# A two-layer MetaFormer on one core: the second layer's order taken from a table of 59 operations by one rule, instead of a repeated period of 34 steps

## The chip, the cores and the metric

The kernel runs on one core of a Trainium2 chip. The time is that of the device for one execution, in microseconds; the number compared is the median of several runs. The engines named below are PE (matrix multiply), DVE (vector), ACT (activations), POOL (GpSimd), and SP, which only issues transfers. Each engine works through its own list of instructions in the order in which the program emitted them, and an instruction whose operands aren't ready stops everything behind it on that engine.

## What is computed

The input is 16 samples of 128 channels by 32 x 32 positions. Cut to what matters:

```python
# layer 0
x = x + linear_attention(ln_c(x))            # GroupNorm, q/k softmax, 4 heads
t = t + stu(ln_t(t))                          # spectral filters over the 1024 tokens: FFT convolutions + 3 taps
# layer 1
h = ln_c(x)                                   # normalize over channels, per position
x = x + relu(bn(conv3x3(relu(bn(conv3x3(h, w1))), w2)) + h)
n = ln_t(tokens(x))                           # normalize over channels, per token
p = softmax(n @ gate_w.T, over tokens)        # 64 experts choose
vals, idx = top_k(p, 8)                       # 8 tokens per expert
pooled = sum over k of vals * n[idx]
out = gelu([pooled, 1] @ weight1) , then @ weight2   # per expert
x = x + scatter_add(out * vals at idx)        # back to the chosen tokens
```

## The kernel before

Layer 0 has two stages (attention and the forward transform for all samples; then the products with the spectral filters, in 16 chunks of 8 frequencies each). Each chunk leaves results in DRAM (`yd`, L839). Layer 1 runs per sample b and is what the change touches. A sample goes through these steps, each a handful of instructions:

- **Inverse transform.** The sample's `y` is loaded from `yd` and its `x` from `xd` (`load`, L960 to L963). POOL forms the even classes (L976, L977), DVE the odd sums, turns and classes (L983 to L1003), PE multiplies by the inverse table `wi` (L1045), and DVE adds the result to x (L1053).
- **First norm.** PE transposes x into PSUM (L149), ACT copies the tile to `tok` (L1059), DVE takes the moments with four bn_stats (L132) from the same PSUM tile, ACT takes logarithm and exponential for the inverse root (L118, L119), POOL refines it and forms the shift (L1020 to L1027), ACT normalizes eight blocks (L141), PE transposes back (L159), and ACT copies the image into a padded tile `pads` (L1070).
- **Two 3 x 3 convolutions**, in a form that computes two output columns from four products. DVE forms four terms (L920). For each half of the rows, PE computes a "middle" pair of products and an "outer" pair (12 matmuls each, L926) into one of three PSUM tiles; ACT shifts (L936), DVE forms sums (L938, L939) and rows (L946, L947). After the first convolution ACT applies the relu into `pads` (L1080); after the second DVE adds the residual and x (L1091, L1093).
- **Second norm and routing.** Tokens again (L1103 for the copy), moments, root, scales, norm, a transpose to channels (L159, L1116). Then once per pair of samples: logits (L1125, L1130), the eight largest (L1135, L1137), marks (L1139), exponential (L1142), gates (L1146), a transpose of the gates (L1156) and the pooling (L1162 to L1171).

The transposes, the inverse transform, the logits and the turned gates share a PSUM tile `big` with two buffers; the products share `pcv` with three. `y` has two buffers, `z`, `zt`, `tok` and the logits tile one, the term tile `v` two, the image two, the relu's image one.

A sample is a Python generator, `convolve_and_route(b)`, that yields at 34 named points. The order is a list `period` of (name, offset): in period p the step `name` of sample p + offset is emitted, so that a period of the steady state holds steps of seven different samples. Its first six entries and the loop:

```python
period = (
    ("first0", 0), ("pooled", -4), ("scales2", -2), ("largest", -3), ("first0o", 0),
    ("norm2", -2), ...
)
for p in range(-2, B + 4):
    for name, d in early if p < 0 else period:
        b = p + d
```

The instructions of these engines keep the order in which they are emitted. In a step, everything stays together: "tokens" is transposes, then ACT's copy, then the moments; "first0" is the middle products, the shift and the sums. After the last sample's pooling the experts' stage begins (L1226 on), whose weights `we` are loaded into buffers that layer 1 gives up (`load_half`).

Of the kernel before, what the change touches and what calls it, by code (L numbers as in the profile page):

```python
# [66 lines left out]
def metaformer_kernel(ctx: ExitStack, tc: tile.TileContext, io: dict, out: bass.AP):  # L67
# [60 lines left out]
    def moments(work, src):  # L128

        bst = work.tile([P, NT, 3], F32, name="bst", tag="bst", bufs=4)  # L130
        for j in range(0, NT, 2):
            nc.vector.bn_stats(  # L132
                bst[:, j : j + 2, :].rearrange("p j s -> p (j s)"),
                src[:, j : j + 2, :].rearrange("p j c -> p c j"),
            )
        return bst[:, :, 1], bst[:, :, 2]
# [27 lines left out]
    with ExitStack() as l0:  # L164
# [6 lines left out]
              for i, n in enumerate((P - JL, JL))]  # L171
# [574 lines left out]
        with ExitStack() as g0:  # L746
# [61 lines left out]
            for c in range(NCH):  # L808
# [27 lines left out]
                for kl in range(JL // RG):  # L836
                    last = c + 1 == NCH
                    j0 = kl * RG + (0 if last else c * JL)
                    nc.sync.dma_start(  # L839
                        yd[last][j0 : j0 + RG].rearrange("g r b x e -> (g r b) (x e)"),  # L840
                        ys[:, kl].rearrange("p x m e -> p (x m e)"),
                    )
# [12 lines left out]
    with ExitStack() as c1:  # L855
# [76 lines left out]
        def conv_middle(v, wt, hf, bias):  # L932

            pc = products(v, wt, hf, (1, 2))
            t = work.tile([P, HR, WT], F32, name="ct", tag="ct")
            nc.scalar.activation(t, pc[:, 0], AF.Identity, bias=bias)  # L936
            sd = work.tile([P, 2, HR, WT], F32, name="cs", tag="cs")
            nc.vector.tensor_tensor(sd[:, 0], pc[:, 1], t, ALU.add)  # L938
            nc.vector.scalar_tensor_tensor(sd[:, 1], pc[:, 1], -1.0, t, ALU.mult, ALU.add)  # L939
            return sd  # L940

        def conv_outer(v, wt, hf, sd):

            pc = products(v, wt, hf, (0, 3))
            r = work.tile([P, 2, HR, WT], F32, name="r", tag="r")
            nc.vector.tensor_tensor(r[:, 0], pc[:, 0], sd[:, 0], ALU.add)  # L946
            nc.vector.scalar_tensor_tensor(r[:, 1], pc[:, 1], -1.0, sd[:, 1], ALU.mult, ALU.add)  # L947
            return r

# [8 lines left out]
        def load(b):  # L958
# [3 lines left out]
            for i, js in enumerate((slice(P - JL), slice(P - JL, P))):  # L962
                (nc.gpsimd if b + i == 0 else nc.sync).dma_start(  # L963
                    yts[b][js].rearrange("p r x e -> p r (x e)"),
                    yd[i][:, :, b].rearrange("j r x e -> j r (x e)"),
                )
# [43 lines left out]
        def convolve_and_route(b):  # L1010

            pr, j = divmod(b, 2)
            p1, p2 = pads[:, b % 2], pads[:, 2]
            g = nc.gpsimd

            def scales(q, e):

                sts = work.tile([P, 5, NT], F32, name="sts", tag="sts")
                r, a, t, mm, nm = (sts[:, i, :] for i in range(5))
                g.tensor_scalar(a, q, 1.0 / C, e, ALU.mult, ALU.add)  # L1020
                log_exp(r, q, 1.0 / C, e)
                g.tensor_tensor(t, r, r, ALU.mult)
                g.tensor_tensor(t, t, a, ALU.mult)
                g.tensor_scalar(t, t, -0.5, 1.5, ALU.mult, ALU.add)
                g.tensor_tensor(r, r, t, ALU.mult)
                g.tensor_scalar(mm, r, -1.0, None, ALU.mult)
                g.tensor_tensor(nm, m, mm, ALU.mult)  # L1027
                return r, nm


            xb = xt[b]
            y = yts.pop(b).rearrange("p r x e -> p (r x) e")
            z = work.tile([P, 12, C], F32, name="z", tag="z", bufs=1)
            even_classes(z, y)
            zt = odd_sums(y)
            yield "classes"
            odd_turns(*zt[1:])
            yield "classes2"
            odd_classes(z, zt[0], zt[2])
            yield "classes3"  # L1040
            px = big()
            for q in range(NQ):
                for r in range(2):
                    zq = y[:, q // 4 + 2 * NM * r, :] if q % 4 == 0 else z[:, 2 * ZQ[q] + r, :]
                    nc.tensor.matmul(  # L1045
                        px[:, q * P : (q + 1) * P], zq, wi[:, q, r, :],
                        start=(r == 0), stop=(r == 1),
                    )
            del y
            if b + 1 < B:  # L1050
                load(b + 1)
            xv = xb.rearrange("p (s q) -> p s q", q=NQ)
            nc.vector.tensor_tensor(xv, px.rearrange("p (q s) -> p s q", q=NQ), xv, ALU.add)  # L1053
            yield "inverse"

            pt = tokens(big())
            transpose_in(pt, xb)
            tok = work.tile([P, NT, C], F32, name="tok", tag="tok", bufs=1)
            nc.scalar.copy(tok, pt)  # L1059
            m, q = moments(work, pt)  # L1060
            yield "tokens"
            r, nm = scales(q, 1e-6)
            yield "scales"
            normalize(tok, tok, r, nm, 0, 2)
            yield "norm0"
            normalize(tok, tok, r, nm, 2, NT)
            yield "norm1"
            px = big()
            transpose_out(px, tok)
            nc.scalar.copy(inner(p1), px.rearrange("p (h w o) -> p o h w", w=WT, o=2))  # L1070
            yield "image"
            v = first.tile([P, 4, HP, WT], F32, name="v", tag="v", bufs=2)
            terms(v, p1, (1, 2, 0, 3))
            yield "terms"
            for hf in range(2):
                sd = conv_middle(v, cw[0], hf, bn[:, 0, 1:2])
                yield f"first{hf}"
                r = conv_outer(v, cw[0], hf, sd)
                yield f"first{hf}o"
                nc.scalar.activation(inner(p2, hf), r, AF.Relu)  # L1080
                yield f"first{hf}r"
            v = first.tile([P, 4, HP, WT], F32, name="v", tag="v", bufs=2)
            terms(v, p2, (1, 2))
            yield "terms2"
            terms(v, p2, (0, 3))
            yield "terms3"
            for hf in range(2):
                sd = conv_middle(v, cw[1], hf, bn[:, 1, 1:2])
                yield f"second{hf}"
                r = conv_outer(v, cw[1], hf, sd)  # L1090
                nc.vector.tensor_tensor(r, r, inner(p1, hf), ALU.add)  # L1091
                xh = xb[:, hf * HALF : (hf + 1) * HALF].rearrange("p (n o) -> p o n", o=2)
# [3 lines left out]
                yield f"second{hf}o"  # L1096


            pt = tokens(big())
            transpose_in(pt, xb)  # L1100
            tt = work.tile([P, NT, C], F32, name="tt", tag="tt", bufs=4)
            toks[b] = tt
            nc.scalar.copy(tt, pt)  # L1103
            m, q = moments(work, pt)
            yield "tokens2"
            r, nm = scales(q, 1e-5)
            yield "scales2"
            normalize(tt, tt, r, nm, 0, 3)
            yield "norm2"
            normalize(tt, tt, r, nm, 3, NT)  # L1110
            yield "norm3"
            pu = big()
            transpose_out(pu, tt)
            tk = work.tile([P, N], F32, name="tk", tag="tk")
            tks[b] = tk
            nc.scalar.copy(tk, pu)  # L1116
            yield "channels"
            if j == 0:
                return

            pl = big()
            for hf in range(2):
                cs = slice(hf * HALF, (hf + 1) * HALF)
                for jj in range(2):
                    nc.tensor.matmul(  # L1125
                        pl[jj * E : (jj + 1) * E, cs], gw, tks[b - 1 + jj][:, cs],
                        start=True, stop=True, skip_group_check=True,
                    )
            lg = work.tile([P, N], F32, name="lg", tag="lg", bufs=1)
            nc.scalar.activation(lg, pl, AF.Identity, bias=gb)  # L1130
            yield "logits"


            top = work.tile([P, TOPK], F32, name="top", tag="top")
            nc.vector.max(top, lg)  # L1135
            lr = work.tile([P, N], F32, name="lr", tag="lr", bufs=1)
            nc.vector.match_replace(lr, top, lg, -3.0e38)  # L1137
            yield "largest"
            nc.vector.tensor_tensor(lr, lg, lr, ALU.not_equal)  # L1139
            ss = work.tile([P, 3], F32, name="ss", tag="ss")  # L1140
            nc.vector.tensor_scalar(ss[:, 0:1], top[:, 0:1], -1.0, None, ALU.mult)
# [251 lines left out]
```

## Time and profile before

| | |
|---|---|
| Time, median of 3 runs | 1379.61 us (1378.31 to 1382.88) |
| PE busy over the span | 1242.8 us, 90% |
| DVE, ACT, POOL busy | 920.6 (67%), 700.1 (51%), 486.7 us (35%) |
| PE's last product of layer 0 / first of layer 1 | ends 679.3 / starts 693.5 us |
| Experts' first matmul | 1270.4 us |
| DMA | 162.98 MB, mean 118 GB/s |

The page is that of one profiled execution; times within it are microseconds from its start. Busy time of an engine is the sum over its instructions, and "idle before" is the time for which an engine stood still ahead of an instruction, with the event that ended it. A share over the whole span mixes the three stages, so stretches of the trace are looked at by themselves.

### The profile page before, as it was taken

The page shows a single profiled execution, that of the slowest core. Times are in us where ns is not written, and L with a number is a line of the kernel's source. Part 1 is how long each engine was busy: PE and PEld are TensorE (multiplying, and loading weights), DVE is VectorE, ACT ScalarE, POOL GpSimd, SP SyncE. Part 2 cuts the span into 40 slices and gives each one's busy share as a digit, 9 for nine tenths or more (in the row PEclk, how much of TensorE's full clock was granted, in tenths as well). Part 3 has the DMA queues.
Part 4 walks back from the last instruction along what each step waited for, and adds up shares of the span by engine and source line. Part 5 has one row for each costly group of instructions (what it writes and reads, how often), then busy time and mean ns, then how long its engine had stood idle before and what let it go on. Part 6 is the DMA issues. An engine that isn't in the chain of part 4 may idle for free.

```text
span 1379.3 us, 33751 instructions
## 1 busy us (share of the span) xinstructions
PE 1242.8 (90%) x14116; PEld 1000.6 (73%) x14116; DVE 920.6 (67%) x1982; ACT 700.1 (51%) x1424; POOL 486.7 (35%) x816
## 2 busy tenths in 40 slices
PE   4889999999989999999659998989998999976885
PEld 4767777777768888888557987878787888852343
DVE  4788878787756766667446877777777767652224
ACT  4777767776556666666213444444454444433111
POOL 2233544546576777777411111111111111100002
PEclk7899999999999999999979999999999999986898
DMA  6015333342443333333662214040404033015895
GB/s 257 16 34 164 110 131 122 123 149 92 154 161 103 126 127 129 129 126 118 215 160 46 47 31 104 5 107 1 107 1 107 1 92 122 16 65 200 314 368 244
DMA packets 87274, 162.98 MB, mean 118 GB/s; under 512 B 5457, under 2 KB 40657, under 8 KB 86737
## 3 DMA queue, kind: packets, MB, share of 16 engines
q1 hardware_dynamic: 86449, 158.27, 34.9%
q0 software_dynamic: 672, 2.56, 0.6%
q8 instruction: 111, 1.82, 0.5%
q14 instruction: 42, 0.34, 0.1%
HBM read 104.18 MB, written 56.62 MB: 117 GB/s over the span
## 4 chain that ended last, share of the span: by engine, by line
PE 34%; DVE 8%; ACT 4%; DMA 2%; issue 1%; POOL 1%; POOLq 0%; SPq 0%; ACTq 0%; DVEq 0%
PE pcv L926 19%; PE big L1045 4%; PE big L149 2%; PE big L159 2%; PE big L1125 1%; PE ph L1233 1%; PE pp L1162 1%; PE peo L1257 1%; PE ph L1226 1%; DMA we<-in_weight 1%; DVE bst L132 1%; ACT tt L141 1%; DVE v L920 1%; DVE lr L1137 1%; ACT lg L1142 1%
## 5 line engine op out<-in xcount | busy, mean ns | idle before, releaser
L926 PE MATMUL pcv<-v,cw 128*128 128x256 f32 x1536 | 347.5, 385 | 1.9 <-DVE v L920 1.9
L926 PEld LDWEIGHTS pcv<-v,cw 128*128 128x128 f32 x1536 | 293.3, 194 | 42.6 <-DVE v L920 2.1
L785 ACT COPY g<-pg 128x512 f32<-128x512 f32 x288 | 153.1, 591 | 101.7 <-PE pg L776 101.7
L783 DVE COPY g<-pg 128x512 f32<-128x512 f32 x224 | 145.9, 687 | 87.4 <-PE pg L776 87.4
L776 PE MATMUL pg<-ph,mst 32*128 32x128 f32 x4096 | 154.2, 286 | 4.5 <-ACT g L785 3.1
L776 PEld LDWEIGHTS pg<-ph,mst 32*128 32x128 f32 x4096 | 129.7, 189 | 30.7 <-issue 25.6
L1020 POOL TENSOR_SCALAR sts<-bst 128x8 f32<-128x8 f32 x32 | 11.9, 371 | 394.5 <-DVE bst L132 394.5
L796 PE MATMUL py<-g,v 128*32 128x128 f32 x4096 | 139.0, 276 | 4.3 <-issue 1.4
L132 DVE BATCH_NORM_STATS2 bst<-big 128x6 f32<-128x256 f32 x256 | 91.4, 419 | 55.7 <-ACT tok L1059 29.3
L796 PEld LDWEIGHTS py<-g,v 128*32 128x32 f32 x4096 | 104.8, 109 | 20.8 <-issue 2.7
L767 POOL TENSOR_TENSOR v<-xc 128x256 f32<-128x256 f32 x128 | 92.0, 746 | 69.0 <-PE py L796 60.0
L141 ACT ACTIVATE tok<-tok,sts 128x128 f32<-128x128 f32 x256 | 103.1, 481 | 5.8 <-DVE sts L375 3.3
L920 DVE TENSOR_TENSOR v<-pads 128x544 f32<-128x544 f32 x128 | 86.2, 725 | 7.9 <-ACT pads L1070 6.4
L618 PE MATMUL big<-u,mu 128*128 128x128 f32 (+4 forms) x384 | 86.0, 380 | 0.0
L936 ACT ACTIVATE ct<-pcv,bn 128x256 f32<-128x256 f32 x64 | 30.0, 469 | 91.7 <-PE pcv L926 91.7
L274 POOL TENSOR_TENSOR xf<-ab 128x256 f32<-128x256 f32 x34 | 24.8, 729 | 132.2 <-DVE ab L241 132.1
L938 DVE TENSOR_TENSOR cs<-pcv,ct 128x256 f32<-128x256 f32 x64 | 27.0, 421 | 65.4 <-ACT ct L936 65.3
L618 PEld LDWEIGHTS big<-u,mu 128*128 128x128 f32 x384 | 56.7, 191 | 18.0 <-issue 15.4
L141 ACT ACTIVATE tt<-tt,sts 128x128 f32<-128x128 f32 x128 | 52.5, 482 | 28.3 <-POOL sts L1027 28.3
L1045 PE MATMUL big<-wi,z 128*128 128x128 f32 x384 | 54.2, 294 | 10.0 <-DVE z L1003 7.1
L551 PE MATMUL big<-wf,ub 128*128 128x256 f32 x256 | 62.0, 385 | 0.2
L149 PEld LDWEIGHTS big<-ident,x 128*128 128x128 f32 x384 | 46.9, 148 | 20.9 <-issue 8.1
(230 smaller groups left out, 2284.4 us busy)
## 6 DMA issues: line engine op xcount, KB each, us to landing
we<-in_weight SPq DMA_DIRECT2D x32, 1024.0 KB
vd<-xf SPq DMA_DIRECT2D x16, 1024.0 KB
xc<-vd SPq DMA_DIRECT2D x64, 256.0 KB
yd<-ys SPq DMA_DIRECT2D x32, 512.0 KB
y<-yd SPq DMA_DIRECT2D x15, 960.0 KB
x<-in_x SPq DMA_DIRECT2D x16, 512.0 KB
mi<-in_M_phi SPq DMA_DIRECT2D x16, 512.0 KB
xd<-x SPq DMA_DIRECT2D x16, 512.0 KB
```

Source lines behind the costliest of these rows:

```text
L132: nc.vector.bn_stats(bst[:, j : j + 2, :].rearrange("p j s -> p (j s)"), src[:, j : j + 2, :].rearrange("p j c -> p c j"),)
L141: nc.scalar.activation(dst[:, j, :], src[:, j, :], AF.Identity, bias=nm[:, j : j + 1], scale=r[:, j : j + 1],)
L149: nc.tensor.transpose(pt[:, j, :], src[:, j * P : (j + 1) * P], ident)
L618: nc.tensor.matmul(self.pa[:, a:hi], mu[:, NF - 1 - si, tap, :], self.u[:, a - tap : hi - tap], start=(tap == 0), stop=(tap == KU - 1),)
L767: nc.gpsimd.tensor_tensor(vv[:, x, 1:, bs], e, o, op)
L776: nc.tensor.matmul(pg[r][:, i], mst[rs, 4 * q + i, :], ph[rs, c, :], start=True, stop=True,)
L783: nc.vector.tensor_copy(dst, src)
L785: nc.scalar.copy(dst, src)
L796: nc.tensor.matmul(py[rows, x, kl, :], v[:, (x * NM + m) * JL + jl, 1 - ri : 3 - ri, :] .rearrange("p k b -> p (k b)"), g[:, ((x * 2 + ri) ...
L920: nc.vector.tensor_tensor(v[:, k], d[i], d[j], op)
L926: nc.tensor.matmul(pc[:, i], wt[:, dy, k, :], v[:, k, hf * HR + dy : hf * HR + dy + HR], start=(dy == 0), stop=(dy == 2),)
L1045: nc.tensor.matmul(px[:, q * P : (q + 1) * P], zq, wi[:, q, r, :], start=(r == 0), stop=(r == 1),)
```

## The change

The generator becomes a class `Routed` with one method for each operation of one engine. What was a step with work on three engines is now taken apart: copies, moments, variance, root, products, shifts, sums and relus are operations of their own. A table gives each operation its engine, a duration in us, a due time, the operations it depends on, and the buffers it opens and closes. Before the program is emitted, `planned` goes through all operations of all 16 samples once: of those whose inputs are done (0.15 us later when they come from another engine) and whose buffers are free, it finds the earliest that can start, and among all that can start within 0.25 us of that one it takes the one with the earliest due time (due + 54.66 per sample). The list, sorted by planned start and then by name, is the order of emission. It is thus no longer periodic: the first and the last samples have an order of their own. The samples' inputs are taken to be there at 0, 4 and 8 us for the first three, and always for the others.

Beside it: `load` of two samples is issued at the beginning and that of sample b + 2 with the inverse of b (before: one, and b + 1); the last write group of `yd` holds two chunks (16 rows) instead of one, so that the load of the first 112 rows doesn't depend on chunk 14; the buffers of the moments' tile go from 4 to 5, of the scales' tile from 2 to 4. The aim is to keep PE supplied, in the middle and at both ends, and to take the moments, which the norm waits for, ahead of the copies. The computation is the same. The core of the diff:

```diff
-        bst = work.tile([P, NT, 3], F32, name="bst", tag="bst", bufs=4)
+        bst = work.tile([P, NT, 3], F32, name="bst", tag="bst", bufs=5)
...
-              for i, n in enumerate((P - JL, JL))]
+              for i, n in enumerate((P - 2 * JL, 2 * JL))]
...
-                    last = c + 1 == NCH
-                    j0 = kl * RG + (0 if last else c * JL)
+                    last = c + 2 >= NCH
+                    j0 = kl * RG + (c - NCH + 2 if last else c) * JL
...
-            pt = tokens(big())
-            transpose_in(pt, xb)
-            tok = work.tile([P, NT, C], F32, name="tok", tag="tok", bufs=1)
-            nc.scalar.copy(tok, pt)
-            m, q = moments(work, pt)
-            yield "tokens"
...
+            def tokens(self):
+                self.pt = tokens(big())
+                transpose_in(self.pt, self.x)
+
+            def stats(self):
+                self.m, self.q = moments(work, self.pt)
+                self.sts = small([P, 5, NT], "sts")
+
+            def copy(self):
+                self.tok = work.tile([P, NT, C], F32, name="tok", tag="tok", bufs=1)
+                nc.scalar.copy(self.tok, self.pt)
...
+        table = (
+            ("even", "POOL", 1.85, -409.2, "", "z", ""),
+            ("odd", "DVE", 1.4, 60, "", "zt", ""),
+            ("odd_turn", "DVE", 0.75, -162.8, "odd", "", ""),
+            ("odd_out", "DVE", 1.4, 308, "odd_turn even", "", "zt"),
+            ("inverse", "PE", 3.5, -181.4, "even odd_out", "big:0", "z"),
+            ("add", "DVE", 1.25, 32, "inverse", "", "big:0"),
+            ("tokens", "PE", 0.88, -255.4, "add", "big:1", ""),
+            ("stats", "DVE", 1.4, 65, "tokens", "", "big:1"),
+            ("copy", "ACT", 1.02, -202.6, "tokens", "tok", "big:1"),
...
+            ("terms", "DVE", 2.6, -242.7, "image_copy", "v:0", ""),
+            ("middle 0", "PE", 2.6, -433, "terms", "cv:0m", "v:0"),
+            ("shift 0", "ACT", 0.48, -171, "middle0", "", ""),
+            ("sums 0", "DVE", 0.74, -165.9, "shift0", "cs:0", "cv:0m"),
+            ("outer 0", "PE", 2.6, -360.9, "terms", "cv:0o", "v:0"),
+            ("rows 0", "DVE", 0.74, -387.6, "outer0 sums0", "r:0", "cv:0o cs:0"),
+            ("relu 0", "ACT", 0.64, -76.6, "rows0", "p2", "r:0"),
...
+            ("terms_middle", "DVE", 1.36, -205.6, "relu0 relu1", "v:1", ""),
+            ("terms_outer", "DVE", 1.36, -37.3, "terms_middle", "", "p2"),
...
+            ("logits", "PE", 1.75, -188.7, "channels_copy -channels_copy", "big:5", "tk -tk"),
...
+            ("pooled_copy", "DVE", 0.3, 242, "pooled", "", "s"),
         )
...
+        buffers = dict(z=1, zt=1, big=2, tok=1, p1=2, v=2, cv=3, cs=2, r=2, p2=1, tt=4, tk=2, lg=1, lr=1, gt=1, s=1)
...
+        order = planned(
+            table, buffers, B, 54.66, lambda b, name: b % 2 == 0 and name in pairs,
+            lambda b: 4.0 * b if b < 3 else 0.0,
+        )
...
+            for b in range(2):
+                load(b)
...
+                if b == B - 1 and name == "inverse":
                     for h in range(5):
                         load_half(h)
-                elif p == B:
+                elif b == B - 1 and name == "rows21":
                     for h in range(5, len(RING)):
                         load_half(h)
+                elif b == B - 1 and name == "logits":
...
+    hop, window, never = 0.15, 0.25, 1e18
...
+        soon = min(starts.values()) + window
+        k = min((k for k, t in starts.items() if t <= soon), key=lambda k: (ops[k][2], starts[k]))
...
+    return [k for _, k in sorted(order)]
```

## The prediction

> **What bounds the kernel now.** I first read the stages: busy time of each engine in stretches of the second layer (the two convolutions and the routing, 692 to about 1270 us). The columns are the stretch, its length, busy time of PE, weight loads, DVE, ACT and POOL with instruction counts, granted clock, DMA share, GB/s.
>
> ```profile
> 671.00:692.00 21.00, 5.62 (x166) 4.47 (x160) 4.77 (x12) 1.12 (x3) 4.74 (x6) 0.81 0.90 298
> 692.00:752.00 60.00, 44.84 (x224) 39.03 (x225) 32.90 (x70) 15.97 (x33) 8.80 (x21) 0.81 0.48 111
> 752.00:820.70 68.70, 68.70 (x387) 61.76 (x385) 56.14 (x123) 32.60 (x73) 12.54 (x41) 1.00 0.17 39
> ...
> 886.70:952.70 66.00, 62.53 (x372) 53.72 (x371) 49.50 (x104) 31.02 (x64) 11.19 (x32) 1.00 0.23 57
> ...
> 1151.70:1200.00 48.30, 45.83 (x262) 38.71 (x262) 29.99 (x60) 24.01 (x49) 6.14 (x21) 0.96 0.27 99
> 1200.00:1268.00 68.00, 47.68 (x231) 34.56 (x231) 29.47 (x56) 22.90 (x40) 2.86 (x14) 0.80 0.30 108
> ```
>
> PE bounds the stage: nothing is free from 752 to 820.7, where no routing runs yet. From 820.7 on a pair of samples takes 66.1 us (the logits matmuls start at 820.73 and, four pairs later, at 1085.21), with DVE busy 49.5 us and ACT 31.0 us. The ends are looser than the middle.
>
> Busy PE is not PE at its peak, so I count what a pair must stream, with the back-to-back spacing in the chain that ended last: 192 convolution matmuls at 0.216 us (24 in 5.18) are 41.4; 64 of the inverse transform at 0.112 (32 in 3.57) are 7.1; 72 transposes at 0.109 are 7.8; logits 1.9, pooling 1.9, pooled 0.1. Sum 60.2 us, **5.9 us less than the period**. Where they go, in the order of time on PE (start, length, and in brackets the idle time before it and its releaser):
>
> ```profile
> 904.32 0.49 PE L159 MATMUL big<-ident,tt 128*128 128x128 f32 x3
> 906.24 1.87 PE L159 MATMUL big<-ident,tt 128*128 128x128 f32 x5 [1.43 <-ACT tt L141]
> ...
> 919.18 0.61 PE L1045 MATMUL big<-wi,y 128*128 128x128 f32 x4
> 920.39 1.60 PE L1045 MATMUL big<-wi,z 128*128 128x128 f32 x12 [0.60 <-DVE z L1003]
> ...
> 923.89 1.09 PE L149 MATMUL big<-ident,gt 128*128 128x128 f32 x8
> 926.09 1.09 PE L149 MATMUL big<-ident,x 128*128 128x128 f32 x8 [1.10 <-ACT gtt L1156]
> ```
>
> PE stands ahead of work that isn't ready while other products could run: 3.1 us of plain gaps, and five transposes that take 1.87 us because each waits for its normalized tile. That is a matter of order, which is what is changed. Last, who waits on the engines beside PE in that pair (waiter, releaser, us, times, longest):
>
> ```profile
> ACT ct L936 <- PE pcv L926: 8.1, 4, 3.7
> DVE cs L938 <- ACT ct L936: 7.7, 4, 3.6
> ...
> DVE bst L132 <- ACT tok L1059: 3.6, 2, 2.0
> ```
>
> DVE's moments wait for ACT's copy of the same PSUM tile; over the layer this line stands at 29.3 us, 16 times.
>
> [...] (all 16 moments of the first norm start after the copy's end, 0.03 us later, at 706.10 for the first). [...] after PE's 14.1 us of idleness before 693.5 the granted clock is 0.50 and inverse matmuls take 0.552 instead of 0.275 us. It makes gaps of several us at both ends dearer than they look.
>
> **The change, part by part.** No matmul, vector or ACT instruction is added or removed; one 8-element POOL operation per norm becomes an operation of its own.
>
> *Order in the middle.* The rule starts, on every engine, what is ready first and breaks near ties (0.25 us) by due time. Its table agrees with the trace: 27.8 us of PE per sample and 4.5 per pair make 60.1 (60.2 measured); a product 2.6 (2.59), terms 2.6 (2.63), moments 1.4 (1.43). PE is the fullest queue, and the table's engines are DVE 49 and ACT 31 per pair, so PE rarely lacks something ready: between a sample's two convolutions lies rows, relu and two terms, 0.74 + 0.64 + 1.36 and hops, some 3.2 us, against 7 us of other PE work per sample. Bounds on the saving are 0 and 5.9 us per pair. I take 3.7, to 62.4 a pair: the waits of the fence above less some new ones. Five pairs (820.7 to 1151.7): **18 us**.
>
> *The end.* From 1151.7 to the experts' first matmul at 1270.4 are 118.7 us. Still to stream: 240 convolution matmuls (51.8), 32 inverse (3.6), 105 transposes (11.4), logits and pooling of three pairs (5.6 + 5.7): 78.4 with the rest. From the last convolution's end (1238.1) to 1270.4 runs one chain, tokens, moments, norm, logits, largest eight, gates, pooling; the order can't shorten it, and I leave it at 32 us, of which 9 stream. Before 1238.1 then, 86.4 us hold 69 of work: 17 lost, since the old period thins out as samples run out. With the last samples interleaved freely I keep 6 of them: **11 us**.
>
> *The start.* The last write group now holds two chunks, 16 rows. Before, GpSimd's bulk load of the first sample waited 8.3 us for chunk 14's store, was issued at 683.4, landed at 692.7; the small load followed chunk 15's store (686.5) and PE began at 693.5. Chunk 13's store was issued at 658.0, so the bulk load can now go out near 672 and land beside the weights (4 MB at the 382 GB/s of 671 to 681, over by about 685). The small load doubles to 128 KB but finds less ahead of it: bounds 0 and 5 us, I take **3.5**. From the first convolution (718.9) to 752 the old order holds 25.2 us of streaming in 33.1; I take **4** of the 8.
>
> *Moments ahead of copies.* At equal planned starts the sort falls to the names, and "copy" comes before "stats"; moments go first only where ACT is busy longer than DVE. The plan lets both overlap, the chip does not: whichever is second is late by 1.0 or 1.4 us against the plan, twice per sample. If DVE is second, its queue (sums and rows of the products, which free the three product banks) stands 1 us; PE has up to two products of 2.6 us queued in free banks meanwhile. Bounds 0 and 2 us per sample.
>
> *Loads the plan doesn't know.* After sample 2 the table thinks every sample's input is there at once. But y has two buffers: sample b+2's load is issued when inverse b has read y, and lands about 8 us later (issued 714.9, DMA full until 723). The rule can put DVE's odd sums of b+2 as early as inverse b's end + 0.15 + 1.85 (even) + 0.15 + 1.4 (odd out), 3.6 us after it and 5 us after the issue. So DVE can stand up to 3 us per sample with sums and rows queued behind it; where DVE is backlogged it costs nothing. Bounds 0 and 3 us per sample. For both leaks together I charge 0.5 us per sample, **8 us**: DVE has 12 us of room in 62, and product banks absorb most of it.
>
> *Five moment buffers, split POOL operation, prefetch of two samples:* nothing. Moments wait on copies, not buffers; POOL is busy 11 of 66 us; y loads were issued at the same event before, SP running ahead to the buffer's release.
>
> Sum: 18 + 11 + 3.5 + 4 - 8 = 28.5, less one for a slow-clock stretch: about 27.5 us off 1379.6, **1352 us**. The experts' stage follows rigidly: four of its first nine weight loads are tied to the last sample's rows, 30 us ahead of pooled in both kernels.
>
> **Rivals.** (1) *DVE becomes the bound.* 49.5 busy, plus 4 of copies and up to 6 of loads per pair is 59.5 of 62. Then the middle keeps its 66 us, and only the ends gain, some 11 us: **1369**. For it: the two leaks above; against: a late DVE no longer waits for loads. (2) *Slower.* A fixed order for all samples, worked out with durations, has no slack written into it; if each sample's stall repeats on PE the pair becomes 68 us, 5 x 2 = 10 lost, and the ends give nothing: **1390**. For it: PE had no gap at all from 752 to 820.7, which the new order can only keep or spoil, and inverse transforms run early take PE from products; against: measured products are no longer than the table's, so PE as the bound queue gives the others slack. (3) *Near the floor:* 61 us a pair (26), 14 at the end, 8 at the start, leaks of 4: 44 off, **1336**.
>
> **Chances.** Forecast 0.58, DVE-bound 0.20, slower 0.14, near the floor 0.08. Range 1334 to 1384, which takes in the first rival and the floor, and cuts through the slower case. Faster by over 0.3% (under 1375.5) is the forecast, the floor and nearly all of the first rival less some scatter: 0.81; same 0.05; slower 0.14.
>
> **What would show it.** Right: logits matmuls some 62.4 us apart per pair; waits of PE on ACT tt L141 and gtt copies gone from the middle; first inverse matmul near 690; less than 10 us of idle PE between 752 and the last convolution; the last convolution's end to the experts' first matmul still near 32 us. The leaks show as DVE's zt operations waiting for the y load and as moments still behind copies (or copies behind moments). Wrong: pairs still 66 apart with DVE over 85% busy or waiting (rival 1), or pairs above 66 with PE idle on DVE's terms or rows (rival 2). A moved start of the experts' stage without a moved end would mean that weight loads bound it, which I take not to be so.

## The result, and the profile after

1323.88 us (median of 4 runs, 1323.63 to 1324.34) against 1379.85 before: a ratio of 0.9592, 95% interval 0.9576 to 0.9609. The kernel is 56 us faster, twice what was forecast and 10 us under the low end of the range. One execution among all those reported below, in the kernel with its end filled, took 1599.0 us at a granted clock of 0.74; it counts as slow and is left out.

The stages of the changed kernel, with the columns of the first view of before (stretch, length, busy time of PE, weight loads, DVE, ACT and POOL, granted clock of PE as a share of full speed, DMA share, GB/s):

```profile
694.00:752.00 58.00, 47.51 (x283) 43.14 (x284) 44.99 (x102) 20.22 (x43) 15.03 (x31) 0.88 0.55 144
752.00:813.80 61.80, 60.04 (x337) 53.27 (x335) 43.93 (x97) 28.07 (x60) 13.20 (x32) 1.00 0.20 52
...
874.50:935.20 60.70, 60.70 (x371) 53.39 (x373) 47.47 (x103) 31.86 (x64) 12.89 (x32) 1.00 0.22 62
...
1117.20:1185.00 67.80, 67.80 (x367) 57.40 (x367) 50.53 (x105) 32.18 (x60) 8.31 (x21) 1.00 0.02 9
1185.00:1217.50 32.50, 19.97 (x126) 13.73 (x124) 12.08 (x24) 16.06 (x30) 3.17 (x14) 0.79 0.62 227
1217.50:1322.00 104.50, 79.91 (x920) 38.63 (x920) 34.08 (x62) 13.61 (x20) 9.42 (x4) 0.94 0.84 322
```

A pair takes 60.7 us, half a microsecond more than the 60.2 counted as PE's streaming work; PE has no gap from 799 to the end of the last product (1187.6). The same place in a pair as was shown of before, in the order of time on PE, carries no bracket any more:

```profile
899.86 1.04 PE L159 MATMUL big<-ident,tt 128*128 128x128 f32 x8
900.73 1.04 PE L149 MATMUL big<-ident,gt 128*128 128x128 f32 x8
901.60 2.76 PE L926 MATMUL pcv<-v,cw 128*128 128x256 f32 x12
904.29 1.97 PE L1242 MATMUL pp<-tt,gtt 128*64 128x128 f32 x32
906.19 1.09 PE L159 MATMUL big<-ident,tok 128*128 128x128 f32 x8
```

The eight channel transposes stream in 1.04 us, since they start when all eight blocks are normalized, and a product of 2.6 us stands between the gates' transposes and the pooling, where before PE waited 1.1 us for ACT's copy.

Where the 57.1 us between the two profiled executions (1379.3 and 1322.2) lie, by the starts of matmuls:

| Stretch | before | after | gain |
|---|---|---|---|
| to the end of layer 0 | 679.3 | 681.3 | -2.0 |
| end of layer 0 to first inverse matmul | 14.1 | 13.5 | 0.7 |
| to the first logits | 127.2 | 119.0 | 8.2 |
| five pairs, first to sixth logits | 331.0 | 303.4 | 27.6 |
| sixth logits to the experts' first matmul | 118.7 | 100.4 | 18.3 |
| experts and output | 109.0 | 104.7 | 4.3 |

Layer 0's end lies between 677.4 and 681.6 in the twelve profiles without added matmuls at that place, whose code there differs at most in loads and stores; so I take its 2 us for scatter.

### The profile page after: what moved, and what is told of

Read it like the earlier page. It is cut to its first block, busy times and chain, and to the rows that moved or that the text cites. A ratio compares the mean times of both kernels' runs of the same rounds, so it can differ in the third digit from the quotient of the medians.

```text
span 1322.2 us, 33734 instructions
## 1 busy us (share of the span) xinstructions
PE 1216.7 (92%) x14116; PEld 990.8 (75%) x14116; DVE 907.2 (69%) x1982; ACT 705.2 (53%) x1424; POOL 503.3 (38%) x816
## 5 line engine op out<-in xcount | busy, mean ns | idle before, releaser
L926 PE MATMUL pcv<-v,cw 128*128 128x256 f32 x1536 | 342.9, 380 | 0.0
L926 PEld LDWEIGHTS pcv<-v,cw 128*128 128x128 f32 x1536 | 286.8, 190 | 42.2 <-issue 5.7
L141 ACT ACTIVATE tok<-tok,sts 128x128 f32<-128x128 f32 x256 | 101.8, 481 | 23.8 <-POOL sts L1001 20.4
L1066 POOL TENSOR_SCALAR sts<-bst 128x8 f32<-128x8 f32 x16 | 6.5, 406 | 235.7 <-DVE bst L132 235.7
L149 PE MATMUL big<-ident,x 128*128 128x128 f32 x384 | 53.6, 286 | 8.5 <-DVE x L1048 3.4
L1115 DVE TENSOR_TENSOR r<-pcv,cs 128x256 f32<-128x256 f32 x64 | 26.9, 420 | 49.0 <-PE pcv L926 48.2
L141 ACT ACTIVATE tt<-tt,sts 128x128 f32<-128x128 f32 x128 | 51.1, 480 | 9.2 <-POOL sts L1001 8.9
```

The costliest lines, as they stand in the source:

```text
L141: nc.scalar.activation(dst[:, j, :], src[:, j, :], AF.Identity, bias=nm[:, j : j + 1], scale=r[:, j : j + 1],)
L149: nc.tensor.transpose(pt[:, j, :], src[:, j * P : (j + 1) * P], ident)
L926: nc.tensor.matmul(pc[:, i], wt[:, dy, k, :], v[:, k, hf * HR + dy : hf * HR + dy + HR], start=(dy == 0), stop=(dy == 2),)
```

## The experiments

Theory A: PE's own order, with DVE's and ACT's operations placed so that its operands are there, makes the gain. Rivals: B, DVE's waits on copies had held PE back; C, the loads at the start; D, a plan passes every delay on to PE. A later question was what in the plan does it: the rule, the lengths or the due times.

The kernel before, measured anew beside the experiments, took 1382.9, 1383.9 and 1383.7 us, 3 to 4 us more than beside the change. So a time below is to be compared with the changed kernel's by the two ratios, or by lengths of stretches inside the traces; a difference of a few us between two times says nothing.

**Moments ahead of copies, alone, in the kernel before.**

```diff
-            nc.scalar.copy(tok, pt)
             m, q = moments(work, pt)
+            nc.scalar.copy(tok, pt)
```
(and the same for `tt`)

> The kernel before with one edit: in both norms the moments are emitted ahead of ACT's copy of the same tile. If the whole gain came from the order of PE's work (theory A), the 41 us of DVE waits on copies go, copies wait for moments instead, and the time stays within 6 us of 1380. If DVE's waits on copies were what held PE back (theory B, a rival), most of the 5.9 us per pair goes and the time falls by 20 us or more, to 1360 or less.

Measured 1373.2, ratio 0.9937 (0.9914 to 0.9961): 9 us off, 64.5 us per pair in four of its five pairs. Between the two expectations. Waits in one pair of it (waiter, releaser, us, times, longest):

```profile
ACT tt L1104 <- DVE bst L132: 8.5, 2, 5.5
...
ACT tok L1060 <- DVE bst L132: 1.3, 2, 0.8
```

The copies now wait for moments, for longer than the moments had waited for them (3.6 and 1.3 us in that pair of before), and still PE gains 1.6 us per pair. Its waits for the second norm (ACT tt L141, 7.1 us over five pairs of the kernel before) are gone there; those for the gates' copy (5.5) remain. The norm needs both, but behind the moments still lie variance, root and scales before it can start, while the copy is needed only then. So B can hold for a sixth of the gain at most, not for the rest.

**The loads and buffers beside the order, alone, in the kernel before** (two chunks in the last write group, two samples loaded at the start, b + 2 with inverse b, five moment buffers).

> The kernel before with the change's parts beside the order: two chunks in the last write group, loads of two samples at the start and of b + 2 with the inverse of b, five moment buffers. Prediction's own step: 3.5 us off, first inverse matmul near 690. Theory A, from the trace of after, where the last store took 7 us instead of 4 beside the earlier bulk load: no change within 2 us, first inverse matmul still 13 to 14 us after layer 0's last matmul.

Measured 1380.0, ratio 0.9984 (0.9973 to 0.9995). The first inverse matmul came 11.1 us after layer 0's last (14.1 before), so the prediction's start step holds here; some 2 us of it (0.7 to 3.7) reach the time. My expectation from the trace of after was wrong.

**The changed kernel with one chunk in the last group.**

> The changed kernel with the write groups of before (one chunk in the last). Theory A: the split gives nothing, 1322 to 1326. If the split is worth the 3.5 us of the prediction: 1327 to 1328.

Measured 1332.6, ratio to before 0.9637 (0.9604 to 0.9669): by the ratios 6 us above the changed kernel, and outside both expectations. The four executions spread over 9 us (1326.9 to 1336.2). In the trace the first inverse matmul comes 0.7 us later after layer 0 and the first logits 1.7 us later after that, so the split is worth about 2.4 us where it acts. The rest lies where it doesn't act: the last chain takes 31.3 us against 30.0, all of it in the last logits (4.7 us against 3.5), and the experts' stage 111.1 against 104.7. That led to the clock (below).

**Moments twice in the changed kernel.**

```diff
-        for j in range(0, NT, 2):
+        for j in (*range(0, NT, 2),) * times:      # times = 2 in layer 1
```

> The changed kernel with layer 1's moments taken twice (the second time over the same result, so the output is the same): DVE gets 1.43 us more twice per sample, 5.7 per pair, and each norm's scales come 1.4 us later than the plan thinks; this exceeds the leak that the prediction charged. Theory A (PE is the bound and DVE has slack): pairs stay within 0.7 us of 60.7, and the time rises by what the ends show, 3 to 6 us. Rival (a plan without slack passes every delay on to PE, or DVE is near its bound): pairs rise by 3 to 6 us and the time by 20 us or more.

Measured 1339.6, ratio 0.9691 (0.9654 to 0.9727); the four executions are two of 1335 to 1336 and two of 1343 to 1345. A pair takes 61.9 us:

```profile
877.10:938.97 61.87, 61.65 (x371) 53.43 (x370) 52.39 (x119) 31.47 (x64) 12.67 (x32) 1.00 0.21 60
```

DVE's busy time rose from 47.5 to 52.4 in it and each norm came 1.4 us later, four times per pair, 5.7 us of delay; 1.2 reached the pair. A fifth passes on: far less than the 3 to 6 us of D, but more than the 0.7 that I allowed under A, so the slack isn't free. Layer 1 as a whole grew by 11 us where I had expected 3 to 6 in all; 3.8 of them lie behind the sixth logits.

**What in the plan does it.** Four kernels with the changed code and another table (it has 64 rows, 17 of them PE's, where the title and two expectations count 59 and 16):

```diff
+        table = [t[:3] + (0.0,) + t[4:] for t in table]          # due times zero: oldest sample first
+        table = [t[:2] + (1.5, 0.0) + t[4:] for t in table]      # and every length 1.5 us
+        table = [t if t[1] in ("PE",) else t[:3] + (0.0,) + t[4:] for t in table]     # PE's due times alone
+        table = [t if t[1] in ("DVE", "ACT", "POOL") else t[:3] + (0.0,) + t[4:] for t in table]   # the others'
         order = planned(
```

> The changed kernel with all due times within a sample set to zero; 54.66 per sample stays, so near ties go to the oldest sample. Lengths, buffers and the rule are the same. If the gain is that of the rule (operations apart, what is ready starts), pairs stay under 62.5 and the time under 1340. If the 59 due times carry it, pairs are above 63 and the time above 1345.

> As the one before, and every operation's length in the table set to 1.5 us: the rule knows neither due times nor lengths, only dependencies and buffers. If lengths matter (a plan is only as good as its durations), pairs are above 66 and the time is 1370 or more. If dependencies and buffers alone do it, pairs stay below 63 and the time below 1345.

> The changed kernel with due times kept only for PE's 16 operations and set to zero for those of DVE, ACT and POOL. Without any, the time was 1377.7. If the gain of the due times lies in which product or transpose PE takes first: 1325 to 1340, pairs near 61. If it lies in what DVE and ACT do first (so that PE's operands are there): 1360 or more, pairs of uneven length.

> The counterpart: due times kept for DVE, ACT and POOL, zero for PE's operations. If the choice of PE carries the gain: 1360 or more. If that of DVE and ACT carries it: 1325 to 1340. If both are about as slow as with none, the due times work only as a set.

| Table | time | ratio to before, 95% | first inverse to experts | a pair, mean |
|---|---|---|---|---|
| (before) | 1379.9 to 1383.9 | 1 | 576.9 | 66.2 |
| no lengths, no due times | 1394.0 | 1.0088 (1.0050 to 1.0125) | 594.3 | 68.4 |
| lengths, no due times | 1377.7 | 0.9951 (0.9936 to 0.9965) | 572.5 | 64.9 |
| lengths, due times of DVE, ACT, POOL | 1353.2 | 0.9784 (0.9750 to 0.9817) | 548.0 | 62.6 |
| lengths, due times of PE | 1336.4 | 0.9654 (0.9618 to 0.9690) | 533.6 | 61.6 |
| lengths, all due times (the change) | 1323.9 | 0.9592 (0.9576 to 0.9609) | 522.8 | 60.7 |

The last two columns are of the one profiled execution, which in the first row lay 7 us above its median. Where only a part of the due times is kept, pairs alternate (42.9 and 80.3 us, 57.4 and 67.8), and the mean is over four of them.

The rule with true lengths and no due times is worth 4 of layer 1's 54 us; the due times carry 50. PE's alone bring 39 of those, which was the one expectation; the others' alone bring 25, between the two that I had set. So neither set suffices and they overlap. The order shows what they change. PE's list at the end of the layer, in the changed kernel and in the one without due times (name.sample; `middle20` and `outer20` are the first half of the second convolution, `middle21` and `outer21` the second half):

```
changed:  middle0.15 outer0.15 middle1.15 channels.13 outer1.15 logits.13 middle21.14 outer21.14 middle20.15
no dues:  middle0.15 pooled.13 outer0.15 outer1.15 channels.14 middle1.15 middle20.15
```

Between a sample's two convolutions lie rows, relu and terms, about 3 us in which that sample has no product. The changed order has kept back two products of sample 14 to fill them, and has two of the sample before at that place in every steady period. Without due times PE has used up sample 14 by then and waits. In the middle of the layer that list fills the place with transposes and inverse transforms of other samples, and PE waits elsewhere: 12.8 us of idle time in five pairs, where the changed kernel has none. Lines of the kernel without due times, on PE:

```profile
1063.14 1.97 PE L1242 MATMUL pp<-tt,gtt 128*64 128x128 f32 x32 [1.10 <-ACT gtt L1235]
1068.79 1.06 PE L159 MATMUL big<-ident,tok 128*128 128x128 f32 x8 [2.54 <-DVE bst L132]
...
1120.45 1.21 PE L159 MATMUL big<-ident,tt 128*128 128x128 f32 x8 [2.43 <-ACT pads L1083]
1182.65 4.54 PE L926 MATMUL pcv<-v,cw 128*128 128x256 f32 x12 [4.96 <-DVE v L920]
...
1222.80 12.31 PE L926 MATMUL pcv<-v,cw 128*128 128x256 f32 x48 [3.50 <-DVE v L920]
```

The last is sample 15's second convolution (48 matmuls left) behind its terms; the one at 1182.65 is its first convolution, whose image came late. The first is a wait of before in another place. The second and third are new: transposes wait until moments, or the copy of an image, have been taken from one of the two `big` buffers; the image copies make almost 7 of the 12.8 us. That the products kept back make the gain is read from these lists and waits; no run moved them alone.

**The clock.** Two kernels aimed at the start and at the half clock. `idle(n)` emits n matmuls of ident on ident into a free product bank, which nobody reads:

```diff
+            idle(100)                # ahead of sample 0's inverse
...
+                        idle(2)      # last sample: behind each channel transpose
+                    idle(64)         # behind its logits
+                    idle(8)          # behind its gates' transposes
```

> The changed kernel with matmuls that nobody reads: 100 of ident on ident ahead of the first inverse transform, and about 90 in the gaps of the last chain (two behind each of the last sample's channel transposes, 64 behind its logits, 8 behind its gates' transposes). The clock theory: inverse matmuls of sample 0 take 0.275 instead of 0.55 us, last logits 1.9 instead of 3.4, gates' transposes 1.0 instead of 1.9, pooling 1.9 instead of 3.7; 4 us at the end and 2 to 4 at the start, 1316 to 1318. If the chains there don't pass through PE, no change; if the added matmuls stand in the way, slower.

Measured 1333.3, ratio 0.9630 (0.9593 to 0.9667): no faster than the changed kernel, by the ratios 5 us slower, though the intervals overlap. The matmuls were as short as expected (sample 0's inverse in sets of 1.50 us per twelve, pooling 1.97 against 3.68 in the changed kernel), but I had mis-sized the filling: each of these instructions is recorded as two matmuls of 0.11 us, so 100 took 22.6 us in a gap of 13 and 64 took 14.6 in a gap of 8, and PE's real work stood behind them: the first inverse matmul came at 704.2 instead of 694.8, and the last chain took 34.8 us instead of 30.0. Its experts' stage took 105.6 us.

```diff
-        for n in range(2):
-            nc.sync.dma_start(cw[n], cwd[n])
...
             for b in range(2):
                 load(b)
+                nc.sync.dma_start(cw[b], cwd[b])
```

> The changed kernel with the two loads of convolution weights (768 KB each) issued behind the loads of samples 0 and 1 instead of ahead of them. If the earlier bulk load gained nothing because the last store and the small load share the DMA engines with those weights: first inverse matmul 3 to 5 us earlier after layer 0, time 1319 to 1321. If the start is bound by something else (the loads of y themselves): within 1 us of 1324. If weights then come late for the first product: slower.

Measured 1323.6, ratio 0.9560 (0.9530 to 0.9591): by the ratios 4 us faster than the changed kernel, with intervals that overlap, so no change is shown. The first inverse matmul did come earlier, 10.3 us after layer 0 instead of 13.5, but the experts' stage took 109.7 us instead of 104.7. Then the weights late and the filling in its right size together, at the end alone and at both places:

```diff
+                        idle(1)      # both: behind each channel transpose of the last sample
+                    idle(30)         # both: behind its logits
+                    idle(4)          # both: behind its gates' transposes
+            idle(40)                 # the second only: ahead of sample 0's inverse
```

> The changed kernel with the convolution weights loaded behind samples 0 and 1, and unread matmuls in the gaps of the last chain alone, fewer than before (an added matmul instruction had run as two, and 64 of them took 14.6 us in a gap of 8): one behind each of the last sample's eight channel transposes, 30 behind its logits, 4 behind its gates' transposes. Clock theory: the last chain from the last product to the experts' first matmul 26 to 28 us instead of 30 to 31, the experts' stage 104 to 106 us instead of 110 as without them, time 1313 to 1317. If the experts' stage has two lengths for another reason than the clock: 109 or more with the clock at 1.00 from its start.

> As the one before, and 40 unread matmul instructions (some 9 us) in PE's gap between the layers. If the half clock of the first 15 us costs what the single matmuls show (inverse of sample 0 and two sets of transposes, 4 us): another 2 to 4 us off. If the start hangs on loads and on DVE, POOL and ACT: no further gain.

Measured 1314.2 (three executions), ratio 0.9501 (0.9469 to 0.9534), and 1314.6, 0.9498 (0.9470 to 0.9527). Both are 9 us below the kernel with late weights alone, which was measured against nearly the same time of before (1383.9, and 1383.7 here). The stretch from the last product to the experts' first matmul, and the 16 us after that, in the kernel with late weights alone and then in the one with the end filled:

```profile
1180.30:1210.90 30.60, 17.88 (x114) 11.49 (x112) 9.98 (x19) 15.19 (x27) 1.78 (x9) 0.73 0.67 239
1210.90:1226.90 16.00, 14.51 (x93) 4.18 (x94) 1.76 (x4) 1.79 (x3) 0.00 (x0) 0.56 0.76 259
```

```profile
1182.30:1209.10 26.80, 22.25 (x203) 18.22 (x203) 9.98 (x19) 15.20 (x27) 1.77 (x9) 1.00 0.75 272
1209.10:1225.10 16.00, 13.87 (x182) 5.77 (x182) 3.30 (x8) 2.39 (x4) 0.00 (x0) 1.00 0.97 337
```

With PE kept busy the granted clock is 1.00 instead of 0.73 and 0.56, the chain is 3.8 us shorter, and the experts get 182 matmuls done in 16 us instead of 93; the stage took 102.3 instead of 109.7. Only the unread matmuls differ between these two, so the clock as the cause of both lengths is shown. The changed kernel had that second gain by itself; its own two stretches, and those of the kernel before:

```profile
1187.50:1217.50 30.00, 17.47 (x115) 11.58 (x113) 9.98 (x19) 15.18 (x27) 1.85 (x9) 0.77 0.67 244
1217.50:1233.50 16.00, 13.82 (x182) 5.82 (x182) 3.31 (x8) 2.39 (x4) 0.00 (x0) 1.00 0.97 334
```

```profile
1238.10:1270.30 32.20, 17.93 (x107) 11.03 (x104) 9.89 (x19) 11.38 (x18) 1.43 (x7) 0.69 0.50 181
1270.30:1286.30 16.00, 14.67 (x89) 4.10 (x89) 1.55 (x3) 1.79 (x3) 0.00 (x0) 0.55 0.77 260
```

So 4 of the 57 us are a clock that was at 1.00 from 0.5 us ahead of the experts' first matmul rather than from 14.3 us after it, and the last logits add 1.2 (3.5 us against 4.7). In all profiles the experts' stage takes 102 to 106 us where it starts at a clock of 1.00 (five kernels) and 109 to 111 where it starts at 0.50 (nine). The plan doesn't set this: the kernel with one chunk in the last group and the one with late weights have the same order here and started at 0.50. So these 5 us are no merit of the order, even if the four executions of the changed kernel agree within 0.7 us; I count them as luck. Filling the gap between the layers added nothing: 1314.6 against 1314.2, with the first product 27.2 us after the first inverse matmul instead of 28.2. The start hangs on loads and on the chain over the other engines: behind the filling PE still waits 0.56 us for the load of y, then 1.35 for DVE's sum with x and 3.25 for ACT's norm.

## Why the prediction was wrong, point by point

The bound, the direction and the place were right: PE bounds the layer, its gaps were a matter of order, most of the gain lies in the middle and at the end, and the last chain stayed (32 us forecast, 30.0 measured). What failed is the size of the terms, nearly all to the same side: the middle, the end and a charge for leaks that did not arise make 25 of the 30 us between forecast and measurement.

- **Order in the middle, 18 us: 27.6 measured.** The bounds were 0 and 5.9 us per pair, and I took 3.7, the waits seen "less some new ones". There were no new waits on PE: 5.5 of the 5.9 went. Behind it stands a reading that failed: "the rule starts, on every engine, what is ready first and breaks near ties (0.25 us) by due time" treats the due times as a detail and lets the rule fill PE because PE is the fullest queue. Run without them, that rule gives 64.9 per pair, 1.3 better than before. It was the due times that brought the pair to the floor. And the reason I gave for PE rarely lacking work (7 us of other PE work against 3.2 us between the convolutions) describes the list without due times, which does wait; the changed one holds back products of the sample before as well. (ACT's lengths in the table make 32.7 us per pair, not 31; nothing hangs on it.)
- **Both leaks, 8 us: about none in the middle.** Both waits exist. In the traces of before and of the changed kernel no moments overlap the copy of their tile, 32 pairs in each: the second of the two starts 0.02 us or more after the first has ended. Copies are emitted ahead of moments in 29 of 32 cases, as the sort by name suggested. But DVE's wait on copies is 4.4 us in the whole layer instead of 41, since other DVE work stands between them; the page row of the moments is now

```profile
L132 DVE BATCH_NORM_STATS2 bst<-big 128x6 f32<-128x256 f32 x256 | 91.1, 417 | 19.5 <-PE big L154 12.1
```

  and no line of layer 1 leads it. Waits of the odd sums on y after the first sample's are 6.9 us in four places, all ahead of the first logits. I had charged 1 us per pair; even a forced delay of 5.7 us per pair costs only 1.2.
- **The end, 11 us: 18.3.** "I keep 6 of the 17": PE kept none of them, its list being full to the last product; the last chain gave 2 more. Of these, 1 is the last sample's moments, which go ahead of its copy here and start 3.0 us after the last product instead of 4.0; 1.2 is the clock in the logits. So "the order can't shorten it" was wrong too, by 1 us.
- **The start, 3.5: 0.7.** The bulk load of y did go out early (676.4 instead of 683.4), and the last store then took longer. Issues on SP and on POOL in the changed kernel:

```profile
676.44 0.72 POOL L945 DMA_DIRECT2D y<-yd  x1
```

```profile
684.34 0.87 SPq L839 DMA_DIRECT2D yd<-ys  x2
691.42 0.64 SPq L945 DMA_DIRECT2D y<-yd  x1
```

  The small load could follow the store after 7.1 us instead of 4.1 (682.4 to 686.5 before). With the convolution weights out of the way the first inverse matmul came 10.3 us after layer 0 instead of 13.5, so these transfers did hold it up; that share was not costed. In the kernel before, the same parts did bring the first matmul 3 us forward (11.1 instead of 14.1), so what they cost depends on what else is under way; on what, no run here separates.
- **To the first logits, 4: 8.2.** The chain to the first product even grew (25.4 to 29.0 us), but behind it PE is nearly full. Some 1.6 us of the gain, by my estimate from the counts of matmuls and the spacings in the prediction, is only work done after the first logits instead of before.
- **Experts, 0: 4.3.** "The experts' stage follows rigidly" was wrong: its length has two values, by the clock at its start. This term is luck, as said above; without it the time would still have been below the range, at about 1329.

Of the rivals, DVE as the bound is refuted by DVE's 47.5 of 60.7 us; a slower kernel is what the table without lengths and due times gives; "near the floor" (61 us a pair, 1336) had the middle and the start nearly right (26 and 8 us forecast, 27.6 and 8.9 measured), sized the end too small (14, 18.3), and charged 4 us for leaks. The weight of 0.58 on half of what the bounds allowed was the mistake of judgement: nothing in the profile spoke for the half.

## What to carry to other kernels

When an order is planned, count what the fullest engine of the stage has to stream. Here that was 60.2 us a pair, and a plan made with true lengths and a due time for each operation came within half a microsecond of it (60.7); plain readiness, even with true lengths, left the old time almost unchanged (1377.7 us). The idle time between dependent stages of one item was covered here by work held back from another item. At an end with little for PE to do, look at the granted clock of the next stage too: 9 us of the time could be had here with matmuls that nobody reads, sized to the gap (1314.2 us against 1323.6); oversized, they brought nothing (1333.3).

## What was not expected of the hardware

After the last chain, in which PE stands still for 8.06 us ahead of the gates' transposes, the clock stayed at 0.50 for 14.3 us of the experts' stage in the kernel before, although PE was busy for 4.00, 4.00 and 3.22 us of the first three stretches of 4 us; in the changed kernel, with a gap of 8.05 us at the same place, the same instructions ran at 1.00 from the first. Busy time alone did not raise it.

In the traces of these two kernels the granted clock changes 26 and 18 times, and only at times that lie whole multiples of 3.41 us apart. The stretches between such times around the experts' first matmul, in the changed kernel (1217.55) and then in the kernel with one chunk (1217.34):

```profile
1213.62:1217.03 3.41, 2.99 (x27) 2.43 (x23) 0.29 (x1) 0.22 (x1) 0.00 (x0) 0.50 0.00 0
1217.03:1220.45 3.42, 3.04 (x25) 0.47 (x24) 0.29 (x1) 0.60 (x1) 0.00 (x0) 1.00 0.94 319
```

```profile
1211.26:1214.67 3.41, 2.31 (x23) 2.29 (x24) 0.00 (x0) 2.29 (x2) 0.00 (x0) 0.50 0.19 77
1214.67:1218.09 3.42, 2.62 (x19) 1.36 (x19) 0.58 (x2) 0.00 (x0) 0.00 (x0) 0.50 0.27 80
1218.09:1221.50 3.41, 3.41 (x20) 0.40 (x16) 0.00 (x0) 0.30 (x1) 0.00 (x0) 0.50 0.81 274
1221.50:1224.91 3.41, 3.41 (x17) 0.32 (x10) 0.00 (x0) 0.30 (x1) 0.00 (x0) 0.50 0.94 283
```

The last pooling stands from 5.0 to 1.3 us ahead of the experts in both. In the changed kernel one such stretch holds 2.7 us of it, and the clock rises at its end. In the kernel with one chunk no stretch holds more than 2.3 us of the pooling, in the kernel before none more than 2.2. In three others that started at 0.50 (weights late, and due times of PE alone and of the others alone) it is 1.9 to 2.1, by my estimate from where the experts' matmuls become shorter in their traces. Stretches filled by the experts' matmuls, such as the last two above, did not raise the clock at first. So where these stretches fall on the pooling goes with the outcome in these six kernels. No run moved them alone, so that this decides is not shown; keeping PE busy ahead of the stage settled it in all three kernels that did so.
